# Seven block products for two tiles' q and k, with block sums on GpSimd

## The chip, the cores and the metric

The kernel runs on one core of a Trainium2 chip. The metric is the device time of one execution in microseconds. Times come from repeated runs; the profile is one further execution, in which every instruction was recorded.

## The reference, cut to what matters

The input x has 16 sequences of 1024 rows of 512 numbers, all fp32. One layer of linear attention and one gated feed-forward layer follow each other, each with a residual and a layer norm:

```python
qkv = x @ Wqkv.T + bqkv
q, k, v = jnp.split(qkv, 3, axis=-1)
q, k = rmsnorm(q, gq), rmsnorm(k, gk)          # then 16 heads of 32, rotated by position
qf, kf = relu(rope(q)), relu(rope(k))
vk  = einsum('bhlp,bhld->bhpd', vpad, kf)      # per sequence; vpad is v and a column of ones
res = einsum('bhpd,bhld->bhlp', vk, qf)
attn = res[..., :-1] / (res[..., -1:] + EPS_LIN)
x = layernorm(x + rmsnorm(attn @ Wout.T + bout, gout))
...
out = sigmoid(xr @ W_r.T) * (square(relu(xk @ W_k.T)) @ W_v.T)
x = layernorm(x + out)
```

Here xr and xk are mixes of each row of x with the row before it.

## The kernel before, in words

The rows are cut into N = 128 tiles of 128 rows, eight tiles to a sequence (a "block" below). Every fp32 matrix product is made of three fp32r products: each operand is split into a high half (a copy to fp32r, on ScalarE) and a low half (operand minus high half, on VectorE or GpSimd), and high x high, high x low and low x high are summed in PSUM. A product of 128 rows, 512 input columns and 512 output columns is therefore 4 x 3 = 12 matmuls of 512 columns.

The first stage walks over the tiles. For each, `slot` (L813; `early`, L775, for the first eight tiles) does this:

- loads the transposed tile xt and splits it (`split_x`, L329: copy L332, subtraction L333 giving xl); loads the plain tile xn and splits it (`split_xn`, L342: L347, L348);
- makes q and k, 12 matmuls each (`proj`, L422, matmul L433), into PSUM banks that ScalarE has filled with the bias before (`seed`, L357, through `seeded`, L160);
- takes the sum of squares on ScalarE (L459) and rotates on VectorE (`rope`, L455: two multiplications with tables, L465 and L466, and an addition with halves swapped, L467). q goes to DRAM (q_d). For k follow the mean square (L474), its power -1/2 on GpSimd (`rsqrt`, L147), the relu as high half kh and as fp32 (L478, L479) and the low half kl (L480);
- adds k's columns up over the block on GpSimd (`add_keys`, L484: acc, L489 and L491), and k-transposed times x on TensorE, 12 matmuls into four PSUM banks that stay open for the block (`add_kx`, L493, L509).

After a block, `finish_a`, `finish_s`, `finish_b` and `finish_c` (L519 to L602) make from these sums the 512x512 matrix m that takes q to the output projection of that sequence, and store it to DRAM (m_d). The rotation tables lie in DRAM (tab_d) and are loaded for each tile into four buffers (`rope_table`, L373, load L386). All loads are issued on SP's queue, in the order of the program.

From tile 30 on, every eighth tile also carries one output tile of the attention layer: q comes back from DRAM (`load_q`), is divided (`part_q`, L229) and transposed (`part_qt`, L244), multiplied with m (`part_m`, L260) and normalized with the residual (`part_y`, L290). Eight output tiles are made so in the first stage; the first four stay in SBUF, the others go to DRAM (x1_d). A block with such a tile is called woven below, the others bare.

The order in the first stage is set by the framework's scheduler, which gives every instruction a place on its engine; `in_order` (L107) fixes an engine's order to that of the program, for TensorE and GpSimd up to tile 7 and for TensorE again from the last tile on.

The second stage starts at L880: it loads the feed-forward weights (`load_w`), transposes four tiles of x at a time (`turn`, L892), mixes neighbouring rows, and runs the three feed-forward products, with the rest of the attention's output tiles between them. It begins with four turns of x tiles 0 to 3 while the last sums of the first stage are finished (L970 to L1021).

Of the kernel before, what the change touches and what calls it, by code (L numbers as in the profile page):

```python
# [22 lines left out]
NQ = 3  # L23
FIRST, STEP = 30, 8
# [9 lines left out]
def kernel(  # L34
# [121 lines left out]


# [37 lines left out]
    def load_m(b, c):  # L195
        n = NC_ * b + c + (2 if b > 0 else 0)
        ms[b, c] = ring("m", n, NC_, 2, [P, 2, DIM], F32R, f"mb{b}{c}")
        nc.sync.dma_start(out=f32(ms[b, c]), in_=m_d[b][:, :, c, :])
# [7 lines left out]
    def load_q(j):  # L206
        qs[j] = tp.tile([P, DIM], F32, tag="q", bufs=3, name=f"q{j}")
        nc.sync.dma_start(out=qs[j], in_=q_d[j])

    def x_tile(j):  # L210

        k = j % 11
        if k < NT:
            return tp.tile([P, DIM], F32, tag="x", bufs=NT, name=f"x{j}")
        if k < 2 * NT:
            return own["x"].tile([P, DIM], F32, tag="x", bufs=NT, name=f"x{j}")
        return tp.tile([P, DIM], F32, tag="xw", bufs=3, name=f"x{j}")

    def load_x(j, src=None, early=False):
        if early and j >= NT:  # L220
            xs[j] = tp.tile([P, DIM], F32, tag="xw", bufs=3, name=f"xw{j}")
        else:
            xs[j] = x_tile(j)
# [5 lines left out]
    def part_q(j):  # L229

# [4 lines left out]
        V.reduce_sum(den, heads(pr), AX.X)  # L235
        rs = rstd_all[:, j, 0:1]
# [7 lines left out]
    def part_qt(j):  # L244
        q = qs.pop(j)
        ps = bank(f"psqt{j}")
        transposes(ps, [q[:, c * P : (c + 1) * P] for c in range(NC_)])
        ps = groups(ps)
        th = wp.tile([P, NC_, P], F32R, tag="qth", bufs=2, name=f"qth{j}")
        tl = wp.tile([P, NC_, P], F32R, tag="qtl", bufs=2, name=f"qtl{j}")  # L250
        S.copy(th, ps)
        V.tensor_sub(tl, ps, f32(th))
# [24 lines left out]
    def layernorm_steps(xt, sm, name):  # L277
# [4 lines left out]
        S.activation(junk(name), xt, AF.Square, bias=nm, accum_out=sq)  # L282
        V.tensor_scalar(sq, sq, 1.0 / DIM, LN_EPS, ALU.mult, ALU.add)
# [10 lines left out]
    def part_y_steps(j, ps):  # L294
# [4 lines left out]
        S.activation(junk(f"y{j}"), ps, AF.Square, accum_out=ss)  # L299
        V.tensor_scalar(ss, ss, 1.0 / DIM, RMS_EPS, ALU.mult, ALU.add)  # L300
# [9 lines left out]
    with ExitStack() as a_ctx:  # L310
# [13 lines left out]

        def load_xt(i):
            xts[i] = wa.tile([P, NC_, P], F32, tag="xt", bufs=2, name=f"xt{i}")
            return nc.sync.dma_start(out=xts[i], in_=xt[i])

        def split_x(i):  # L329
            xh[i] = wa.tile([P, NC_, P], F32R, tag="xh", bufs=2, name=f"xh{i}")  # L330
            xl[i] = wa.tile([P, NC_, P], F32R, tag="xl", bufs=2, name=f"xl{i}")
# [10 lines left out]
        def split_xn(i):  # L342

# [3 lines left out]
            S.copy(h, w)  # L347
            V.tensor_sub(l, w, f32(h))  # L348
            xn[i] = h, l

        w_qk = {h: ca.tile([P, NC_, 2 * DIM], F32R, name=f"wqk_{h}") for h in "hl"}
# [21 lines left out]
        def rope_table(i, j):  # L373
# [4 lines left out]
            for n in (1, 0):  # L378
                if i == 2 and n == 1:

                    tb = tp.tile([P, DIM], F32, tag="x", bufs=NT, name=f"tab{j}{n}{i}")
                else:
                    tb = wa.tile([P, DIM], F32, tag=f"tab{j}{n}", name=f"tab{j}{n}{i}")
# [38 lines left out]
        def proj(i, j, by_part=False):  # L422
# [3 lines left out]
            cols = slice(j * DIM, (j + 1) * DIM)  # L426
# [5 lines left out]
            for n, ((a, b), c) in enumerate(order):  # L432
# [3 lines left out]
                    rhs=w_qk[b][:, c, cols],  # L436
# [16 lines left out]
        acc, ros, sums = {}, {}, {}  # L453

        def rope(i, j, ps):  # L455

            if j == 0:
# [5 lines left out]
            r = wa.tile([P, DIM], F32, tag=f"ro{j}", bufs=1 + j, name=f"ro{j}{i}")  # L463
            t2 = wa.tile([P, DIM], F32, tag="t2", name=f"t2{j}{i}")
            V.tensor_mul(t2, ps, tab.pop((i, j, 1)))  # L465
            V.tensor_mul(ps, ps, tab.pop((i, j, 0)))  # L466
            V.tensor_add(halves(r), halves(ps), halves(t2)[:, :, ::-1, :])  # L467
            if j == 0:
                q_d[i] = dram.tile([P, DIM], F32, name=f"q_d{i}")
                nc.sync.dma_start(out=q_d[i], in_=r)  # L470
                return

            ss = sums.pop(i)
            V.tensor_scalar(ss, ss, 1.0 / DIM, RMS_EPS, ALU.mult, ALU.add)  # L474
            rsqrt(rstd_all[:, i, :], ss)
            kh = tk.tile([P, DIM], F32R, tag="kh", bufs=2, name=f"kh{i}")
            kl = tk.tile([P, DIM], F32R, tag="kl", bufs=2, name=f"kl{i}")
            S.activation(kh, r, AF.Relu, scale=rstd_all[:, i, 1:2])  # L478
            S.activation(r, r, AF.Relu, scale=rstd_all[:, i, 1:2])  # L479
            V.tensor_sub(kl, r, f32(kh))  # L480
            state[i] = kh, kl
            ros[i] = r

        def add_keys(i):  # L484

            b, t = divmod(i, 8)
            if t == 1:
                acc[b] = tx.tile([P, DIM], F32, tag="acc", name=f"acc{b}")
                G.tensor_add(acc[b], ros[i - 1], ros[i])  # L489
            if t > 1:  # L490
                G.tensor_add(acc[b], acc[b], ros[i])  # L491

        def add_kx(i):  # L493

            kh, kl = state.pop(i)
            h, l = xn.pop(i)
            b, t = divmod(i, 8)
            if t == 0:
# [6 lines left out]
            if t == 7 and i < N - 1:  # L505

                order = [(three[n], c) for c in range(NC_) for n in (0, 1, 2)]
            for (n, a, r), c in order:
# [4 lines left out]
                    start=(t == 0 and n == 0),  # L513
                    stop=(t == 7 and n == 2),
# [4 lines left out]
        def finish_a(b):  # L519

            kx = tx.tile([P, NC_, NC_, 2, P], F32R, tag="kx", name=f"kx{b}")
            for c, ps in enumerate(ps_kx.pop(b)):
                S.copy(kx[:, c, :, 0, :], groups(ps))
                V.tensor_sub(kx[:, c, :, 1, :], groups(ps), f32(kx[:, c, :, 0, :]))  # L524
            fin[b] = kx

        def split_keys(b):
            a = acc.pop(b)
            m = te.tile([P, 2, DIM], F32R, tag="m", bufs=2, name=f"ma{b}")
            S.copy(m[:, 0, :], a)  # L530
            V.tensor_sub(m[:, 1, :], a, f32(m[:, 0, :]))
            return m

        def finish_s(b, m=None):

            m = split_keys(b) if m is None else m
# [672 lines left out]
```

## Time and profile before

| | us |
|---|---|
| median of 3 runs | 2704.09 (2704.01 to 2704.91) |
| the profiled execution's span, first to last instruction | 2703.0 |
| first stage, up to the last of k's products with x | about 1197 |
| busy: VectorE | 2172.3 |
| busy: ScalarE | 1881.4 |
| busy: GpSimd | 697.4 |

The page names the engines PE (TensorE matmuls), PEld (its weight loads), DVE (VectorE), ACT (ScalarE), POOL (GpSimd) and SP (which issues the DMAs). A busy time is the time in which at least one of the engine's instructions was running, so two instructions that overlap count once. A group's row reads: line, engine, operation, output <- inputs, shapes, count | busy time, mean duration in ns | idle time of the engine just before, and what ended it. In a row of a window of time, each engine's busy time is followed by its number of instructions, then come the granted TensorE clock, the busy share of the DMA engines and GB/s. A row of the timeline starts with the start and the duration in us.

### The profile page before, as it was taken

How to read it: one execution, taken by the hardware profiler on the slowest of the kernel's cores; microseconds unless marked ns; L12 is line 12 of the kernel's file. 1: busy time of each engine (PE TensorE's matmuls, PEld its weight loads, DVE VectorE, ACT ScalarE, POOL GpSimd, SP SyncE). 2: the span in 40 equal slices, each digit the busy share in tenths (PEclk: the TensorE clock that was granted, in tenths of full speed). 3: DMA queues.
4: the chain of work that ended last, by engine and by line, in shares of the span. 5: the costliest groups of instructions: out<-in, count | busy, mean ns of one | idle time of the engine just before them, and what ended most of it. 6: DMA issues, size and time to landing. Idle time of an engine off the chain costs nothing.

```text
span 2703.0 us, 40210 instructions
## 1 busy us (share of the span) xinstructions
PE 2687.1 (99%) x12572; PEld 2231.5 (83%) x12572; DVE 2172.3 (80%) x4884; ACT 1881.4 (70%) x3820; POOL 697.4 (26%) x800
## 2 busy tenths in 40 slices
PE   9999999999999999999999999999999999999998
PEld 7888888888888888887888888888888888888887
DVE  8888888877887788776888888888888888888874
ACT  6666666666666566657787777778777777777775
POOL 5222222222222222234322222222222222222221
PEclk9999999999999999999999999999999999999999
DMA  7788787877777778754232322223132222313210
GB/s 260 238 266 260 260 268 259 264 231 232 229 232 229 255 248 254 245 197 147 92 119 59 109 94 93 85 90 116 59 109 94 89 90 91 113 59 110 74 55 36
DMA packets 232159, 433.28 MB, mean 160 GB/s; under 512 B 24693, under 2 KB 25205, under 8 KB 231945
## 3 DMA queue, kind: packets, MB, share of 16 engines
q1 hardware_dynamic: 231508, 430.05, 49.5%
q8 instruction: 99, 1.62, 0.2%
q14 instruction: 116, 0.94, 0.1%
q10 hardware_dynamic: 436, 0.66, 0.1%
HBM read 314.19 MB, written 116.42 MB: 159 GB/s over the span
## 4 chain that ended last, share of the span: by engine, by line
PE 62%; DVE 1%; ACT 1%; DMA 0%; issue 0%; POOL 0%; POOLq 0%; SPq 0%; DVEq 0%; ACTq 0%
PE psr L183 13%; PE psv L183 13%; PE psk L183 12%; PE psy L183 12%; PE psk L433 3%; PE psq L433 3%; PE pskx L509 3%; PE pst L168 2%; PE psqt L168 2%; PE pskv L556 0%; PE psm L598 0%; DMA q<-q_d 0%; DVE x L1089 0%; DVE mixk L905 0%; PE pskv L564 0%
## 5 line engine op out<-in xcount | busy, mean ns | idle before, releaser
L183 PE MATMUL psk<-mkh,w_k 128*128 128x512 f32 x1024 | 332.6, 396 | 0.8 <-DVE kx L524 0.7
L183 PE MATMUL psv<-w_v,kah 128*128 128x512 f32 (+1 forms) x1032 | 321.8, 393 | 0.0
L183 PE MATMUL psr<-w_r,mrh 128*128 128x512 f32 x1024 | 319.9, 398 | 0.7 <-ACT r L958 0.7
L183 PE MATMUL psy<-mb,qth 128*128 128x512 f32 x1024 | 320.0, 389 | 0.0
L491 POOL TENSOR_TENSOR acc<-acc,ro 128x512 f32<-128x512 f32 x96 | 155.8, 1623 | 268.3 <-ACT ro L479 211.3
L183 PEld LDWEIGHTS psy<-mb,qth 128*128 128x128 f32 x1024 | 191.9, 188 | 39.6
L183 PEld LDWEIGHTS psk<-mkh,w_k 128*128 128x128 f32 x1024 | 191.2, 188 | 40.1 <-DVE kx L524 1.0
L183 PEld LDWEIGHTS psr<-w_r,mrh 128*128 128x128 f32 x1024 | 189.3, 189 | 38.3 <-ACT r L958 1.1
L183 PEld LDWEIGHTS psv<-w_v,kah 128*128 128x128 f32 x1032 | 188.9, 188 | 36.4
L921 POOL TENSOR_TENSOR mkl<-mixk,mkh 128x512 fp32r<-128x512 f32 x127 | 166.2, 1309 | 186.4 <-ACT mkh L919 186.4
L147 POOL TENSOR_TENSOR rstd_all<-ss,mhalf 128x2 f32<-128x2 f32 x128 | 91.1, 712 | 473.2 <-DVE ss L474 465.1
L433 PE MATMUL psq<-wqk_h,xh 128*128 128x512 f32 x512 | 200.7, 392 | 0.7 <-ACT wqk_h L671 0.6
L183 PE MATMUL psv<-w_v,kal 128*128 128x512 f32 (+1 forms) x516 | 200.7, 389 | 0.0
L433 PE MATMUL psk<-wqk_h,xh 128*128 128x512 f32 x512 | 199.0, 390 | 0.9 <-ACT psk L360 0.9
L183 PE MATMUL psy<-mb,qtl 128*128 128x512 f32 x512 | 199.8, 390 | 0.0
L183 PE MATMUL psk<-mkl,w_k 128*128 128x512 f32 x512 | 199.8, 390 | 0.0
L433 PE MATMUL psq<-wqk_l,xh 128*128 128x512 f32 x512 | 198.9, 389 | 0.0
L433 PE MATMUL psq<-wqk_h,xl 128*128 128x512 f32 x512 | 198.8, 389 | 0.0
L433 PE MATMUL psk<-wqk_h,xl 128*128 128x512 f32 x512 | 198.8, 389 | 0.0
L433 PE MATMUL psk<-wqk_l,xh 128*128 128x512 f32 x512 | 198.8, 389 | 0.0
L183 PE MATMUL psr<-w_r,mrl 128*128 128x512 f32 x512 | 197.2, 395 | 0.0
L147 POOL TENSOR_TENSOR yrs<-yss,mhalf 128x1 f32<-128x1 f32 x128 | 70.1, 548 | 392.6 <-DVE yss L300 286.6
(203 smaller groups left out, 7165.9 us busy)
## 6 DMA issues: line engine op xcount, KB each, us to landing
tab<-tab_d SPq DMA_DIRECT2D x480, 256.0 KB
xt<-in_xt_dram SPq DMA_DIRECT2D x128, 256.0 KB
xn<-in_x_dram SPq DMA_DIRECT2D x128, 256.0 KB
q_d<-ro SPq DMA_DIRECT2D x128, 256.0 KB
m_d<-m SPq DMA_DIRECT2D x64, 512.0 KB
mb<-m_d SPq DMA_DIRECT2D x64, 512.0 KB
q<-q_d SPq DMA_DIRECT2D x128, 256.0 KB
out_dram<-x SPq DMA_DIRECT2D x127, 256.0 KB
```

Of the source, the lines that this page charges most:

```text
L147: G.tensor_tensor(dst, src, mhalf[:, 0 : src.shape[1]], ALU.pow)
L168: T.matmul(ps[:, n * P : (n + 1) * P], lhsT=b, rhs=ident, is_transpose=True, start=(n == 0), stop=(n == NC_ - 1), skip_group_check=True,)
L183: T.matmul(ps, lhsT=a[u][:, rows], rhs=b[w][:, cols], start=(afresh and c == 0 and k == 0), stop=(c == n - 1 and k == 2), skip_group_check ...
L433: T.matmul(ps, lhsT=a[i][:, c, :], rhs=w_qk[b][:, c, cols], start=(not seeds and n == 0), stop=(seeds and n == 3 * NC_ - 1), skip_group_ch ...
L491: G.tensor_add(acc[b], acc[b], ros[i])
L509: T.matmul(ps_kx[b][c], lhsT=a[:, c * P : (c + 1) * P], rhs=r, start=(t == 0 and n == 0), stop=(t == 7 and n == 2),)
L921: (V if by_v else G).tensor_sub(ml, m, f32(mh))
```

## The change

Two tiles a and b (of the same block) are taken together. Their transposed rows are each cut into two halves of 256 input columns (a1, a2 of tile a; b1, b2 of tile b, the names the diff gives to b's are contained in its sums), and the weights into q's and k's columns by the same two halves of input columns. The eight block products (two tiles, two halves, q and k; each six matmuls of 512 columns) become seven, p1 to p7, over sums and differences of the blocks.

- The weights' sums are made once, in tiles 2 and 3, on GpSimd (`mix_weights`), and split in tiles 3 to 6 (`split_weights`).
- For each pair GpSimd makes four block sums s1 to s4 and the low halves of all seven left operands, 128x256 each; ScalarE makes the high halves in seven copies.
- Three of the seven results are needed in more than one place: ScalarE copies z (p7) to SBUF (`z_out`) and the running sum to a second bank (`y_seed`), and VectorE makes three additions (`a_seed`: two, `k2_add`: one). The k of tile b is finished in SBUF and rotated there.
- The tables use one ring of five buffers in place of four single ones and come in the order q of a, k of b, q of b, k of a.
- The order of the whole first stage from tile 8 on is written out by hand: `pair` gives every step a time, and the steps are traced sorted by it. TensorE's order is fixed to that from tile 8 on.
- The output tile of a woven block now comes one block later in parts: q and m are loaded for each of them (`load_m(..., f"w{j}")`), and all eight go to DRAM and are loaded back at the start of the second stage, behind w_k and before w_r. One q tile, not three, is prepared ahead of the second stage, and several tiles change their place in SBUF.

```diff
-NQ = 3
-FIRST, STEP = 30, 8
+NQ = 1
+SOLO = 8
+WOVEN = 6
...
-                    tb = wa.tile([P, DIM], F32, tag=f"tab{j}{n}", name=f"tab{j}{n}{i}")
+                    tb = wa.tile([P, DIM], F32, tag="tab", bufs=5, name=f"tab{j}{n}{i}")
...
+        def mix_weights(c):
+            q1, k1, q2, k2 = (stage[j, n] for n in (c, c + 2) for j in range(2))
+            G.tensor_sub(q1, k1, q1)
+            G.tensor_sub(k1, k2, k1)
+            G.tensor_sub(k2, k2, q1)
+            G.tensor_sub(q2, q2, k2)
...
+        def block_sum(i, n):
+            a, b = xts[i], xts[i + 1]
+            one, two = slice(0, 2), slice(2, NC_)
+            u, v, op = {
+                "s3": (a[:, one, :], b[:, one, :], G.tensor_sub),
+                "s1": (b[:, one, :], b[:, two, :], G.tensor_add),
+                "s2": (parts.get((i, "s1")), a[:, one, :], G.tensor_sub),
+                "s4": (a[:, two, :], parts.get((i, "s2")), G.tensor_sub),
+            }[n]
+            t = parts[i, n] = wa.tile([P, 2, P], F32, tag="part", bufs=3, name=f"part{n}{i}")
+            op(t, u, v)
+
+        def split_block_steps(i, n):
...
+            S.copy(t[:, 0], src)
+            yield
+            G.tensor_sub(t[:, 1], src, f32(t[:, 0]))
+
+        def block_product(ps, blk, rhs, afresh=False):
+            order = [(u, w, c) for c in range(2) for u, w in ((0, "h"), (0, "l"), (1, "h"))]
+            for n, (u, w, c) in enumerate(order):
+                T.matmul(ps, lhsT=blk[:, u, c, :], rhs=rhs(w, c), ...)
...
+            def p7():
+                me["z"] = bank(f"psk{b}")
+                block_product(me["z"], blk("s3"), t_(3), afresh=True)
+            def p1():
+                block_product(first[a, 0], blk("a1"), lambda w, c: w_q[w][:, c, :])
+            def p2():
+                block_product(first[a, 0], blk("a2"), lambda w, c: w_q[w][:, 2 + c, :])
+            def p6():
+                block_product(me["y"], blk("s2"), t_(2))
+            def p5():
+                block_product(me["a"], blk("s1"), t_(1))
+            def p4():
+                block_product(me["y"], blk("a4"), t_(4))
+            def p3():
+                block_product(me["a"], blk("s4"), lambda w, c: w_k2[w][:, c, :])
+            def z_out():
+                me["k2"] = rope_tile(b, 1)
+                S.copy(me["k2"], me["z"])
+            def y_seed():
+                me["y"] = bank(f"psq{b}")
+                S.copy(me["y"], first[a, 0])
+            def a_seed():
+                me["a"] = bank(f"psk{a}")
+                V.tensor_add(me["a"], me["y"], b_qk[:, DIM : 2 * DIM])
+                V.tensor_add(me["y"], me["y"], me["k2"])
+            def k2_add():
+                V.tensor_add(me["k2"], me["k2"], me["a"])
...
+            at(t, p7)
+            t += 6 * U
+            at(t, z_out)
+            if was is not None:
+                at(t, was["p3"])
+                t += 6 * U
+            at(t, p1)
...
+            at(t, p6)
+            t += 6 * U
+            ty2 = t
+            at(t, a_seed)
+            at(t, kx_two)
+            t += (12 if r == 0 else 8) * U
...
+            at(t, p5)
+            t += 6 * U
+            ta2 = t
+            at(t, k2_add)
+            steps_at(rope_k_b(), t + 0.75, t + 0.8, t + 1.5, t + 2.2)
+            at(t, p4)
+            t += 6 * U
+            steps_at(rope_q_b(), t + 0.05, t + 1.6, t + 2.2, t + 2.95)
...
+            ts = t + 12 * U
+            steps_at(rope_k_a(), ts + 0.05, ts + 1.2, ts + 1.8, ts + 2.5)
...
+                at(t0 + 1.4, block_sum, n, "s3")
+                steps_at(later(split_block_steps, n, "s3"), t0 + 2.1, t0 + 2.5)
...
+        for i in range(SOLO, N, 2):
+            t = pair(i, t)
...
+            for _, _, fn, args in sorted(events, key=lambda e: e[0:2]):
+                fn(*args)
...
         load_w("k", cb)
+        for j in range(NT):
+            load_x(j, src=x1_d[j])
+        load_w("r", cb)
...
+        add_kx(N - 1)
         for c in range(3):
             turn(0, c, c)
...
-        add_kx(N - 1)
+        add_kx(N - 2)
```

In the diff, U = 0.2267 is the time in us that `pair` gives to one matmul, r is the pair's place in its block (0 to 3), and `kx_two` are the products of k with x of an earlier tile.

## The prediction

> **What bounds the kernel now.** I read the busy table of the page first, then the chain, then the wait list and the busy windows of the attention stage.
>
> ```profile
> span 2703.0 us, 40210 instructions
> ...
> PE 2687.1 (99%) x12572; PEld 2231.5 (83%) x12572; DVE 2172.3 (80%) x4884; ACT 1881.4 (70%) x3820; POOL 697.4 (26%) x800
> ```
>
> ```profile
> 2628.76 10.88 PE psk L183 x48
> 2674.24 10.88 PE psr L183 x48
> ```
>
> TensorE is busy all the way. The chain's rows give the price of one matmul of 512 columns: 10.88/48 = 0.2267 us. Work taken from TensorE is therefore worth its whole time, as long as another engine does not become the bound. For the attention stage the windows of two blocks of eight tiles answer that. The starts of the ksv copy (L541) give the block's period: 75.4 us where an output tile is woven in, 71.8 to 72.3 where none is.
>
> ```profile
> core 0: us, PE busy (x) PEld busy (x) DVE busy (x) ACT busy (x) POOL busy (x), PEclk, DMA share, GB/s
> 391.20:466.60 75.40, 75.40 (x351) 63.02 (x350) 62.67 (x117) 48.73 (x103) 18.04 (x17) 1.00 0.79 262
> 1062.20:1134.50 72.30, 72.30 (x336) 60.44 (x335) 57.34 (x101) 43.82 (x95) 17.43 (x15) 1.00 0.75 237
> ```
>
> TensorE has no gap at a granted clock of 1.00. VectorE is next: 62.7 of 75.4 us (83%) and 57.3 of 72.3 (79%). ScalarE has 35% left, GpSimd 76%, the DMA engines a fifth. Between 300 and 1000 us the wait list has 1.9 us in all in which matmuls or their weight loads waited for VectorE, so VectorE's idle fifth is real cover today.
>
> **The change part by part.** *Matmuls.* For each of 60 pairs seven products of six matmuls replace eight. The program orders hold 11004 and 10644 matmuls of 512 columns: 360 fewer, 360 x 0.2267 = 81.6 us. A block loses 24, or 5.4 us: TensorE needs 66.6 us (bare) or 70.0 (woven).
>
> *VectorE's own work.* Prices from the woven block:
>
> ```profile
> L480 DVE TENSOR_TENSOR kl<-ro,kh 128x512 fp32r<-128x512 f32 x8 | 7.0, 880 | 3.2 <-ACT ro L479 3.2
> ...
> L466 DVE TENSOR_TENSOR psk<-psk,tab 128x512 f32<-128x512 f32 x8 | 5.5, 691 | 0.0
> ...
> L348 DVE TENSOR_TENSOR xnl<-xn,xnh 128x512 fp32r<-128x512 f32 x8 | 5.5, 687 | 2.9 <-ACT xnh L347 2.9
> ...
> L333 DVE TENSOR_TENSOR xl<-xt,xh 128x512 fp32r<-128x512 f32 x8 | 5.5, 684 | 0.5 <-ACT xh L332 0.5
> ```
>
> One operation shows as 0.69 us, but neighbours overlap: L465 to L466 start 0.60 us apart, so each adds about 0.61 to the busy sum. Per block the eight xl subtractions leave for GpSimd (-4.9) and twelve additions come in (two to seed, one to finish, in each of four pairs: +7.3). Without contention a bare block then needs 57.3 + 2.4 = 59.7 us. The woven window also holds three weight splits (1.9) that fall in other blocks after the change: 62.7 - 1.9 + 2.4 = 63.2.
>
> *GpSimd's work and what it does to VectorE.* Per pair there are four block sums and seven low halves, all 128x256; no row shows this form. The memsets of 512 and 256 columns show how GpSimd scales:
>
> ```profile
> L698 POOL MEMSET sel_g<- 128x512 f32 x1 | 0.5, 528 | 0.0
> ...
> L697 POOL MEMSET sel_b<- 128x256 f32 x1 | 0.3, 315 | 0.0
> ```
>
> About 0.1 is fixed, so 1.29 us at 512 columns (L489, L491 undisturbed) makes 0.70 at 256; the ends are 0.64 (half) and 1.29 (all fixed). Per block: 44 x 0.70 + 8 x 1.29 (acc) = 41 us in which GpSimd reads two SBUF operands, 59% of 70 us; with the powers about 47. GpSimd itself has room. The trouble is what two rows of the timeline show:
>
> ```profile
> 501.44 1.29 POOL L491 TENSOR_TENSOR acc<-acc,ro 128x512 f32<-128x512 f32 x1 [2.83 <-ACT ro L479]
> ...
> 502.05 1.24 DVE L233 SCALAR_TENSOR_TENSOR pr<-q,ksb 128x512 f32<-128x512 f32 x1 [3.10 <-DMA q<-q_d]
> ...
> 513.04 0.69 DVE L480 TENSOR_TENSOR kl<-ro,kh 128x512 fp32r<-128x512 f32 x1 [1.39 <-ACT ro L479]
> 513.14 1.75 POOL L491 TENSOR_TENSOR acc<-acc,ro 128x512 f32<-128x512 f32 x1 [2.43 <-ACT ro L479]
> ```
>
> A VectorE operation with two SBUF operands that starts inside a GpSimd one is stretched (0.69 to 1.24), and the other way round GpSimd is (1.29 to 1.75). In 31 such kl starts the stretch is what GpSimd had left, less 0.14 us; operations with one operand in PSUM (L467) keep 0.69 inside the same spans. After the change 34 VectorE operations of a bare block have two SBUF operands (per pair two kl, two xnl, and the three of k's rotation that now starts in SBUF; six others), 37 of a woven one. Hit at random: 0.59 x (mean rest 0.425 - 0.14 = 0.285) = 0.17 us each, 5.7 and 6.2 us a block. Ends: what the two blocks carry today (1.7 and 2.2, their stretches in the trace), and every operation finding GpSimd at work, 0.285 each.
> The Trainium skill ("SBUF — State Buffer", Who interferes with whom) says that the later of the two fully blocks, and counts any GpSimd instruction that reads SBUF. By that a hit would cost the whole rest, 0.59 x 0.425 = 0.25 us, and the sum below would come out at 2712 us, a little slower than now; the rows end 0.14 us sooner, and xnl starts inside the small powers (L147) are not stretched at all (0.69), so I go by the rows.
>
> VectorE's demand: bare 59.7 - 1.7 + 5.7 + 1.2 (weight splits) = 64.9; woven 63.2 - 2.2 + 6.2 = 67.2. That is 97% and 96% of TensorE's need, where today's is 83%.
>
> *VectorE's idle time in its order.* The five table buffers are a ring, so the second table of the pair's last rotation may load only when the first of k's rotation before it has been read. Six VectorE operations (6 x 0.61 = 3.7 us) lie between, and a table took 4.4 us from issue to its sixteenth completion mark (median of 344 between 300 and 1100 us; nine in ten under 5.8): 0.7 us idle a pair; on SP the xn and xt loads and q's store queue behind the waiting table, each with some us to spare. kl waited 0.5 us per tile for ScalarE (37.9 us over 76); with a later VectorE I keep 0.2 a pair. A woven block also loads 2 MB of m again (mb landed in 6.6, not 4.4): 2.2 more. So 3.6 and 5.8 us a block. A late VectorE next holds the seeding additions, and behind them TensorE's products five and four, whose cover is 8 to 12 matmuls (1.8 to 2.7 us).
> Block: 64.9 + 3.6 = 68.5 (TensorE 66.6: 1.9 lost); 67.2 + 5.8 = 73.0 (70.0: 3.0 lost). Seven bare and eight woven blocks: 13 + 24 = 37 us.
>
> *Once only.* Before the first pair, TensorE waits for the square of tile 7's k (0.59 + 0.19), ss 0.16, the power 0.70, a block sum 0.70 and a 256-wide copy 0.40, then for a low half: 3 us. Eight more GpSimd subtractions (8 x 1.29) in tiles 2 and 3 outrun the 8.6 us tile by under 2 us: 1 us. At the end the first turns need four tiles from DRAM, queued on SP behind 2 MB of w_k; the kernel shows the same kind of wait today at the next turn:
>
> ```profile
> 1233.82 0.33 PE L168 MATMUL pst<-ident,x 128*128 128x128 f32 x1 [2.64 <-DMA x<-x_d]
> ```
>
> Here w_k landed 4.4 to 6.7 us after its issue, 1 MB more at 255 GB/s is 4 us, and some 22 to 34 matmuls (5.0 to 7.7 us) cover it: 2 to 6, taken as 4. Together 8 us. The block sums' own chain, ScalarE's seven narrow copies (for two wide ones and one seed fewer) and four more stores of x are hidden: ScalarE is at 65% and all of it is a pair ahead; without that cover a low half late by 0.7 us stops TensorE in each product.
>
> Sum: 2703.0 - 81.6 + 37 + 8 = 2666. The median lies 1.1 us over the profiled span: 2667.
>
> **The rivals.** *All of it hides:* GpSimd's operations fall where VectorE works on PSUM, at 0.10 us or less per operation VectorE stays inside TensorE's time. 2703 - 81.6 + 8 + 1.1 = 2630. For it: today TensorE waits 1.9 us in 700 for VectorE, although kl already meets acc often. Against it: 96% leaves little room to place anything.
> *The shared read decides:* in blocks, the loss is 7 x (34x - 3.8) + 8 x (37x - 3.2) = 534x - 52 us for x us per operation. From x = 0.24 on the 73.6 us left are eaten; at 0.285, every operation meeting GpSimd, the loss is 100: 2730, slower. For it: GpSimd waiting behind one VectorE operation goes next, so k's three in a row can each pay. Against it: GpSimd still rests for a third of the time.
> *The tables decide:* the DMA share rises from 0.79 to about 0.91 in woven blocks (2.1 MB more on 19.8, in 73 us), above the 0.85 that a block reached (279 GB/s, no stall). If tables land 0.7 us later, 2.8 us a block, 42 us: 2709, no change.
> That the change does not remove the matmuls is excluded by the counts.
>
> **How the numbers follow.** Forecast (2640 to 2695) 0.47; all hides 0.22; shared read 0.22; tables 0.09. The time is the forecast's, 2667. Its own range is 2640 to 2695; the range of 8 in 10 reaches into both sides, 2628 to 2722. A measurement here tells 0.2% (5.4 us) from no change. Faster: 0.47 + 0.22 + 0.02 of the tables = 0.71; within: 0.05 of the tables and 0.02 of the shared read = 0.07; slower 0.22.
>
> **What would show it.** TensorE's matmuls of 512 columns fewer by 360; VectorE over 90% busy up to about 1150 us, kl, xnl and k's rotation at means well over 0.69 us, PSUM operations still at 0.69; block periods near 68.5 and 73; TensorE waiting for VectorE's seeding additions. VectorE under 88% with gapless blocks would be the first rival; means over 0.95 us for two-SBUF operations the second; long waits of VectorE on tab the third. Wrong outright: TensorE waiting on GpSimd's low halves in each product.

## The result and the profile after

The changed kernel is slower, by 6%. The profiled execution is the fastest of its four (2863.0 us).

| | before | after |
|---|---|---|
| median, us | 2704.18 (4 runs) | 2870.52 (4 runs, 2863.01 to 2878.52) |
| ratio, 95% interval | | 1.0614 (1.0592 to 1.0636) |
| span of the profiled execution | 2703.0 | 2861.2 |
| start to the first ksv copy | 96.7 | 105.6 |
| mean period of the next six blocks (bare after the change) | 74.2 | 86.3 |
| mean period of the eight after them (woven after the change) | 74.1 | 81.7 |
| period of the last block | 73.7 | 90.8 |
| from there to the end | 1494.8 | 1493.2 |

The periods are those of the ksv copies' starts (L631 now). Of 158 us more in the span, 133 lie in the fourteen blocks, 17 in the last one, 9 at the start. The changed kernel's page, its span and its busy line:

```profile
span 2861.2 us, 40565 instructions
...
PE 2681.5 (94%) x12212; PEld 2171.1 (76%) x12212; DVE 2420.0 (85%) x4953; ACT 1936.5 (68%) x4068; POOL 1274.5 (45%) x1468
```

The 360 matmuls are gone (12572 to 12212 records), and TensorE, busy 99% of the span before, stands still for 6% of a longer one. The windows of a bare and of a woven stretch of the changed kernel:

```profile
200.00:600.00 400.00, 341.56 (x1445) 267.30 (x1445) 341.17 (x488) 220.68 (x504) 250.77 (x272) 0.95 0.67 215
700.00:1200.00 500.00, 447.77 (x1990) 352.62 (x1989) 469.27 (x720) 306.50 (x706) 336.41 (x373) 1.00 0.75 239
```

In the woven stretch VectorE is busy 94%, and little more fits in. In the bare one nothing is: TensorE and VectorE are both at 85%, ScalarE and GpSimd at 55 and 63%. So two things are to be explained: VectorE's larger work, and blocks in which every engine waits. Where TensorE stops is told by the changed kernel's list of waits, TensorE's alone, from 100 to 1340 us (total, times, longest):

```profile
PE psq L997 <- ACT psq L1077: 55.2, 51, 3.3
PE pskx L584 <- DVE kl L548: 32.7, 21, 2.3
PE psm L700 <- DVE m L705: 22.0, 16, 3.1
PE psk L997 <- DVE ro L1085: 14.5, 8, 1.9
PE psm L700 <- DVE ro L521: 9.4, 14, 0.7
```

Before the change the same list held 2.1 us (to 1210 us). (Counted from one matmul's start to the next, less its own 0.23 us, the first line is 65 us and the second 36; the expectations below use that count.) The longest line is a wait that the prediction does not name: p2 adds to the bank out of which ScalarE's copy (`y_seed`, L1077) has just begun to read. The timeline of a woven pair, rows of several engines, shows what comes before that stop:

```profile
909.09 0.69 DVE L1085 TENSOR_TENSOR ro<-ro,psk 128x512 f32<-128x512 f32 x1
...
909.57 0.74 POOL L990 TENSOR_TENSOR blks<-parts,blks 128x256 fp32r<-128x256 f32 x1 [1.86 <-ACT blks L988]
...
909.81 1.05 DVE L516 TENSOR_TENSOR t<-ro,tab 128x512 f32<-128x512 f32 x1
...
910.39 1.07 POOL L978 TENSOR_TENSOR parts<-xt 128x256 f32<-128x256 f32 x1
...
910.95 1.05 DVE L518 TENSOR_TENSOR ro<-ro,tab 128x512 f32<-128x512 f32 x1
...
911.42 1.19 POOL L990 TENSOR_TENSOR blks<-parts,blks 128x256 fp32r<-128x256 f32 x1
...
912.04 1.11 DVE L521 TENSOR_TENSOR ro<-ro,t 128x512 f32<-128x512 f32 x1
...
912.68 1.07 POOL L978 TENSOR_TENSOR parts<-parts,xt 128x256 f32<-128x256 f32 x1
...
913.08 0.70 DVE L534 TENSOR_SCALAR ss<-ss 128x2 f32<-128x2 f32 x1
...
913.86 0.70 POOL L148 TENSOR_TENSOR rstd_all<-ss,mhalf 128x2 f32<-128x2 f32 x1
...
914.59 0.72 ACT L541 ACTIVATE kh<-ro,rstd_all 128x512 fp32r<-128x512 f32 x1 [0.42 <-POOL rstd_all L148]
...
915.22 0.58 ACT L1077 COPY psq<-psq 128x512 f32<-128x512 f32 x1
...
915.85 0.50 PE L997 MATMUL psq<-wq_h,blka 128*128 128x512 f32 x1 [0.45 <-ACT psq L1077]
```

Two things are to be seen. From 909.8 on VectorE and GpSimd take turns: each operation starts inside one of the other engine and ends 0.54 to 0.61 us after that one's end, so all are 1.05 to 1.19 us long instead of 0.69 and 0.73. And the rows are one chain: p5 has ended at 909.1, and k2's addition, the rotation, the sum, the root, kh, the copy (which stands behind kh in ScalarE's queue) and p2 follow one another over 6.8 us. The next pair's p5 ended at 930.5, 14.6 us after p2 began, some 11 of them matmuls at 0.2267 us (3.4 us lie at half clock). There the chain is back where it began, after 21.4 us, and goes round again. Such a closed chain is called a ring below. A quarter of a block's period, the time that a pair has, is 21.6 us (bare) or 20.4 (woven).

### The profile page after: what moved, and what is told of

Same layout as the page of the kernel before. It is cut to its first block, busy times and chain, and to the rows that moved or that the text cites. A ratio compares the mean times of both kernels' runs of the same rounds, so it can differ in the third digit from the quotient of the medians.

```text
span 2861.2 us, 40565 instructions
## 1 busy us (share of the span) xinstructions
PE 2681.5 (94%) x12212; PEld 2171.1 (76%) x12212; DVE 2420.0 (85%) x4953; ACT 1936.5 (68%) x4068; POOL 1274.5 (45%) x1468
## 4 chain that ended last, share of the span: by engine, by line
PE 53%; DVE 1%; DMA 0%; issue 0%; ACT 0%; POOL 0%; POOLq 0%; SPq 0%; DVEq 0%; ACTq 0%
PE psr L188 12%; PE psk L188 12%; PE psv L188 12%; PE psy L188 11%; PE pst L173 2%; PE psqt L173 2%; PE pskx L584 1%; PE psq L997 0%; DMA x<-x_d 0%; DMA w_k<-w_dk 0%; PE psk L997 0%; PE pskv L651 0%; DVE pr L246 0%; DVE t L516 0%; PE psm L700 0%
## 5 line engine op out<-in xcount | busy, mean ns | idle before, releaser
L990 POOL TENSOR_TENSOR blks<-parts,blks 128x256 fp32r<-128x256 f32 x240 | 209.7, 874 | 217.0 <-ACT blks L988 215.6
L188 PE MATMUL psy<-mb,qth 128*128 128x512 f32 x896 | 280.0, 389 | 0.0
L997 PE MATMUL psq<-wq_h,blka 128*128 128x512 f32 x480 | 179.8, 415 | 56.7 <-ACT psq L1077 56.7
L148 POOL TENSOR_TENSOR rsa<-sqa,mhalf 128x1 f32<-128x1 f32 x128 | 79.6, 622 | 304.7 <-DVE sqa L304 293.8
L541 ACT ACTIVATE kh<-ro,rstd_all 128x512 fp32r<-128x512 f32 x128 | 92.7, 725 | 163.0 <-DVE ro L521 110.0
L188 PEld LDWEIGHTS psy<-mb,qth 128*128 128x128 f32 x896 | 168.0, 188 | 34.8
L148 POOL TENSOR_TENSOR rsf<-sqf,mhalf 128x1 f32<-128x1 f32 x128 | 70.2, 555 | 265.6 <-DVE sqf L304 240.4
L584 PE MATMUL pskx<-kl,xnh 128*128 128x512 f32 x512 | 149.7, 400 | 32.7 <-DVE kl L548 32.7
L188 PE MATMUL psy<-mb,qtl 128*128 128x512 f32 x448 | 174.8, 390 | 0.0
L988 ACT CAST blks<-parts 128x256 fp32r<-128x256 f32 x240 | 97.7, 407 | 108.1 <-PE psk L997 67.3
```

The costliest lines, as they stand in the source:

```text
L148: G.tensor_tensor(dst, src, mhalf[:, 0 : src.shape[1]], ALU.pow)
L188: T.matmul(ps, lhsT=a[u][:, rows], rhs=b[w][:, cols], start=(afresh and c == 0 and k == 0), stop=(c == n - 1 and k == 2), skip_group_check ...
L584: T.matmul(ps_kx[b][c], lhsT=a[:, c * P : (c + 1) * P], rhs=r, start=(t == 1 and n == 0), stop=(t == 8 and n == 2),)
L988: S.copy(t[:, 0], src)
L990: G.tensor_sub(t[:, 1], src, f32(t[:, 0]))
L997: T.matmul(ps, lhsT=blk[:, u, c, :], rhs=rhs(w, c), start=(afresh and n == 0), stop=(n == len(order) - 1), skip_group_check=True,)
```

## The experiments

All times stand beside 2870.5 for the changed kernel. The kernel before was run again beside each experiment, with medians of 2703.4 to 2704.2.

### First four: move the copy, move a load, leave GpSimd out

e1_p1_first makes p1 the first product of the pair, ahead of p7, so that the copy has 12 to 16 matmuls of cover:

```diff
+            at(t, p1)
+            t += 6 * U
             at(t, p7)
             t += 6 * U
...
             ta3 = t
-            at(t, p1)
-            t += 6 * U
             tx1 = t
             at(t, y_seed)
```

> Each pair now begins with the first block product (into the first tile's q bank) and makes the seventh after it; all the work is done, nothing else is moved. ScalarE's copy of the bank after the first product then lies under 12 to 16 matmuls (2.7 to 3.6 us) instead of none to 4. Theory A (TensorE loses the time in waits put newly into its fixed order): the 65.1 us that the second product waited for this copy, 52 times, go to under 10, and with some of the stops the half-clock stretches, 71.7 us of them before 1400 us, become fewer; 2870.5 falls by 65 to 95 us, to 2775-2805. Rival B (VectorE, slowed by GpSimd's reads, is the bound, and TensorE's stops only show its lateness): the wait moves from this copy to VectorE's kl, m and k2 sums, the time falls by under 20 us, to 2850 or more.

Measured: 2914.8 us (1.0786, 1.0765 to 1.0808), 44 slower. Both theories fall as they were put. The same stop grew with all its cover, in the list of waits of this run (TensorE, 100 to 1340 us):

```profile
PE psq L997 <- ACT psq L1077: 75.2, 44, 3.5
PE pskx L584 <- DVE kl L548: 42.7, 21, 2.3
```

In 34 of these 44 cases kh, ahead of the copy in ScalarE's queue, had waited for GpSimd's root. The place of p1 was not what made the copy late.

e2_xn_later:

```diff
-            steps_at(xn_b, t + 0.45, t + 2.8)
-            at(t + 2.85, load_xn, a)
+            steps_at(xn_b, t + 2.8, t + 4.4)
+            at(t + 4.45, load_xn, a)
```

> The split of the second tile's x (ScalarE's copy and VectorE's subtraction) is placed 2.35 and 1.6 us later in each pair, and the load that follows it 1.6 us later; all the work is done. Its load is issued only 3 to 5.5 us before its use now, and VectorE, which works in order, sits in the subtraction behind it. Theory A: ScalarE's wait for this load (49.9 us, 39 times between 200 and 1200 us) goes to under 15 us, the waits of the m products for VectorE's m subtraction (24.6 us) and part of those for kl (36.1 us) go with it; the time falls by 20 to 60 us, to 2810-2850. Rival B (VectorE's busy time is the bound, the order of its work is not): VectorE does the same work, the time stays within 10 us of 2870.

Measured: 2870.7 (1.0611, 1.0596 to 1.0627). No change in the time, but ScalarE's wait for the load did not go either (50.4 us from 200 to 1200 us; 49.9 in the changed kernel). So the run does not tell what that wait is worth.

e3_no_gpsimd:

```diff
-            t = parts[i, n] = wa.tile([P, 2, P], F32, tag="part", bufs=3, ...)
-            op(t, u, v)
+            parts[i, n] = u
...
-            G.tensor_sub(t[:, 1], src, f32(t[:, 0]))
...
-                    lhsT=blk[:, u, c, :],
+                    lhsT=(none if u else blk[:, 0])[:, c, :],
```

> GpSimd's block work is left out: the four block sums are replaced by the block they begin with, and the low halves of all seven blocks by one block of zeros made once; TensorE, ScalarE, VectorE and the transfers do as much as before. Theory A with the slow reads as one of its causes: VectorE's additions and subtractions from two SBUF tiles (kl 1255, xnl 1060, k's three steps 981 to 1049 ns between 400 and 1100 us) fall to 0.70-0.80 us, VectorE's busy time before 1400 us by 80 to 130 us, and the stops for kl, m, k2 and the rotation (about 100 us) go to under 35; the copy's 65 us stay; 2870.5 falls to 2755-2800. Rival B (this contention alone decides): the time falls to 2650-2690. Rival C (contention is small, the order of work decides): the additions get faster but the time falls by under 40 us, to 2830 or more.

Measured: 2823.6 (1.0441, 1.0421 to 1.0462). xnl and k's steps do fall to 0.68-0.69 us and VectorE's busy time in a block from 75-77 to 65-66, but the time hardly follows. The s3 cast now reads x directly and waits for its load, and what waits behind it on ScalarE is again the copy. This run's waits of ScalarE (200 to 1200 us) and of TensorE (100 to 1340 us):

```profile
ACT blks L989 <- DMA xt<-in_xt_dram: 63.2, 42, 4.9
```

```profile
PE psq L998 <- ACT psq L1078: 99.4, 43, 5.3
```

The edit took one cause away and, by these lines, made another, so it tells only that VectorE's pace and the time are not the same thing.

e4_both has the first two edits.

> The first and the second edit together (first product first; split of the second tile's x later); all the work is done. Theory A: the gains add up, with some more from the clock, 2720-2775; if the half clock comes from the stops, under 25 us of it are left before 1400 us. Rival B (VectorE bound): 2840 or more.

Measured: 2912.6 (1.0767, 1.0751 to 1.0783): e1 again.

### Second four: ScalarE's order

e5_copy_first puts the copy ahead of kh by a dependency:

```diff
             S.activation(kh, r, AF.Relu, scale=rstd_all[:, i, 1:2])
+            if copied:
+                not_before(last_of(mybir.EngineType.Activation), copied[0])
...
                 S.copy(me["y"], first[a, 0])
+                copied[:] = [last_of(mybir.EngineType.Activation)]
...
-            steps_at(kb, t + 0.9, t + 1.0, t + 3.2, t + 6.5)
+            steps_at(kb, t + 0.9, t + 1.0, t + 4.2, t + 6.5)
```

> Made after the first four runs, which put the copy's lateness on what stands ahead of it in ScalarE's queue: in 41 of the late cases of the changed kernel (50.0 us) it is kh of the pair before, which waits for GpSimd's inverse root. Here ScalarE's copy of the first product is ordered ahead of that kh; all the work is done, nothing else is moved by hand. Theory A (ScalarE's order): the second product's wait for the copy falls from 65 us to under 20, the time by 35 to 75 us, to 2795-2835. Rival B (VectorE's lateness is the bound, the copy is where it happens to show): kh and kl come later by what the copy gained, the stops for kl grow from 36 us by 30 or more, and the time stays at 2850-2885.

Measured: 2943.7 (1.0889, 1.0868 to 1.091), slower than either theory. The stop did leave the copy, and came back larger (TensorE's waits, 100 to 1340 us):

```profile
PE pskx L586 <- DVE kl L550: 63.1, 55, 3.0
PE pskx L586 <- ACT kh L541: 45.4, 22, 3.6
...
PE psq L999 <- ACT psq L1079: 15.1, 14, 1.6
```

kh one copy later, with the next split of x slipped in ahead of kl, makes each pair 1.2 us longer (73 us in 60). A path that answers to a delay like that seems to have no slack.

e6_blocks_after (e5, and three casts later):

```diff
-                steps_at(later(split_block_steps, n, "s2"), ty2 + 0.1, ty2 + 1.1)
-                steps_at(later(split_block_steps, n, "s1"), ta2 + 0.1, ta2 + 1.0)
-                steps_at(later(split_block_steps, n, "s4"), t + 0.6, t + 1.0)
+                steps_at(later(split_block_steps, n, "s2"), t + 0.1, t + 0.5)
+                steps_at(later(split_block_steps, n, "s1"), t + 0.15, t + 1.05)
+                steps_at(later(split_block_steps, n, "s4"), t + 0.6, t + 1.35)
```

> As the run before, and the casts of the blocks s2, s1 and s4 are placed after the last product of the pair; ScalarE sits in front of their buffers (86 us of waits for TensorE's products between 200 and 1200 us) with what is queued behind them. All the work is done. Theory A (any wait in ScalarE's queue comes out at TensorE): 5 to 30 us less than the run before. Rival (those waits are slack): within 6 us of the run before; or slower by 5 to 20 us, where the low halves, now three on GpSimd at once, hold up the inverse root.

Measured: 2949.1 (1.0897, 1.0877 to 1.0917), e5 within its spread. ScalarE's waits for block buffers are slack.

e7_no_gpsimd_copy_first is e3 with e5's dependency, for the casts too.

> The run without GpSimd's block work again (low halves and sums left out), with the copy ahead of kh and of the block casts, which there waited for x. The 113 us of waits for the copy should go to under 25. Theory A (ScalarE's order and VectorE's slowed operations together make the whole loss): 2650-2710, the chain of TensorE work nearly closed before 1340 us. Rival C (there is a third cause, as in transfers or banks): 2750 or more. Rival B (contention alone): the same as without the order, 2810-2830.

Measured: 2850.2 (1.054, 1.0519 to 1.0561). In the count of the expectations the copy's waits went from 113 to 15 us, as expected; 63 us for kl came in their place. VectorE does much the same work in a block here (63 and 65 us) as in e13 below (66 and 67), which is 73 us faster: with nearly the same work of VectorE the time differs, so the order and the waits count.

e8_p1_and_copy is e1 with e5's dependency and the casts of s3 and a1 after the copy (t0 + 4.2 and 4.4 for t0 + 2.1 and 2.6).

> The first product made first, the copy ahead of kh, and the casts of s3 and a1 placed after it; all the work is done. Theory A: the copy then has 12 to 16 matmuls and nothing ahead that waits for GpSimd; its wait is under 10 us, and the time 10 to 40 us under the run with the copy first alone, 2765-2815. Rival B: as the run with the first product first, 2880 or more, with the stops at kl.

Measured: 2866.9 (1.0596, 1.0578 to 1.0614), the changed kernel's time, with 81 us of stops at kl (same count) for the 65 at the copy. The stop that was taken from TensorE at one place came back at another.

### Third four: shorten the ring

e9_kx_after_p6 (e10: with e5's order besides, kl kept ahead of the split; e11: on e8's order):

```diff
-            at(t, next, kx_one)
-            at(t + 8 * U, next, kx_one, None)
-            t += 12 * U
...
             at(t, p6)
             t += 6 * U
             ty2 = t
-            at(t, a_seed)
+            at(max(t, tq + 2.65), a_seed)
+            at(t, next, kx_one)
+            at(t + 8 * U, next, kx_one, None)
+            t += 12 * U
...
             at(t, kx_two)
...
```

> After eight runs a new theory. Followed back from TensorE, the changed kernel's chain of waits between 200 and 600 us is TensorE for only 25%, against 88% before; it runs in a ring from pair to pair: p5, VectorE's k2 addition, the rotation, the sum, GpSimd's root, ScalarE's kh (and, behind it, the copy that p2 waits for), VectorE's kl, TensorE's key products, p6, p5 of the next pair. Here the twelve key products of the second tile stand after p6 instead of before it, which takes p6 and the products woven in ahead of it out of the ring; all the work is done. Theory L (the ring's length is the pair's time): the stops for kl go from 36 to under 12 us, but the ring through the copy is left, so the time falls by 10 to 50 us, to 2820-2860. Rival B (VectorE's sum of work): within 12 us of 2870.

> As the run before, with the copy ordered ahead of kh, and kh, k and kl of the second tile ordered ahead of the next split of x (which had slipped in front of them in the run with the copy first alone); all the work is done. Both ways round the ring are then shorter. Theory L: 2740-2815. Rival B: 2850 or more. If the order alone made the earlier run slow and there is no ring, this is where the copy's 65 us come back: 2790-2810, and the run before shows no gain.

> As the run with the first product first, the copy ahead of kh and the casts later (2867 us), with the twelve key products after p6; all the work is done. There the stops had moved to kl (81 us) and kh (25 us). Theory L: these go to under 30 together, the time to 2730-2800, the lowest of this call. Rival B: 2850 or more.

e12_no_root:

```diff
+            rk = mhalf[:, 0:1] if i > SOLO and i % 2 else rstd_all[:, i, 1:2]
-            S.activation(kh, r, AF.Relu, scale=rstd_all[:, i, 1:2])
+            S.activation(kh, r, AF.Relu, scale=rk)
...
```

> The changed kernel, with kh and k of each pair's second tile scaled by a constant instead of the inverse root (the norm of that tile is left out); all other work is the same, the root is still made. This takes the wait for the sum and for GpSimd's root, 1 to 2 us, out of the ring and out of ScalarE's queue in front of the copy. Theory L: 1.0 to 1.5 us less in each of 60 pairs, 2780-2815. Rival B (VectorE's work, or GpSimd's reads by themselves): less than 15 us, 2855 or more.

| | us | ratio, interval | bare block | woven block |
|---|---|---|---|---|
| e9 | 2843.2 | 1.0517 (1.05 to 1.0535) | 80.0 | 83.1 |
| e10 | 2848.0 | 1.0531 (1.0515 to 1.0547) | 80.8 | 83.4 |
| e11 | 2841.6 | 1.0504 (1.0486 to 1.0521) | 79.1 | 84.8 |
| e12 | 2832.9 | 1.0477 (1.0456 to 1.0498) | 80.2 | 81.9 |

In e9 to e11 the woven tiles' q is turned before it is divided, which changes their part of the output but not the work. All four gain 22 to 38 us. A bare block is 5.5 to 7.2 us shorter, a woven one 0.2 to 3.1 us longer. So the ring's length counts in the bare blocks; e12 takes the root out of the ring and out of ScalarE's queue in front of the copy at once, and does not part the two. What was expected of e10 to e12 (55 us and more) was too much, since the woven half of the stage gains nothing. In e12 VectorE is busy 93% of a woven block, which leaves little to gain; in e9 to e11 it is 88 to 89%, and what holds their woven blocks is not shown.

### Last three: the reads alone

e13_thin keeps every wait, the order and GpSimd's time, and takes the wide reads away:

```diff
-            op(t, u, v)
+            G.memset(t, 0.0)
+            G.memset(t, 0.0)
+            op(t[:, :, 0:4], u[:, :, 0:4], v[:, :, 0:4])
...
-            G.tensor_sub(t[:, 1], src, f32(t[:, 0]))
+            G.memset(f32(t[:, 1]), 0.0)
+            G.memset(f32(t[:, 1]), 0.0)
+            G.tensor_sub(t[:, 1, :, 0:4], src[:, :, 0:4], f32(t[:, 0, :, 0:4]))
```

> The changed kernel, in which each of GpSimd's eleven block operations of a pair is replaced by two fills of the same tile and the subtraction or addition of 4 columns of each 128: it waits for what it waited for and takes about its 0.7 us, but reads next to nothing (the block sums and low halves are left out but for 4 columns). Theory R (VectorE's additions from two SBUF tiles, 0.9 to 1.35 us instead of 0.69, are the main loss): kl to 0.85-1.0 (GpSimd's key additions still read), xnl and k's three steps to under 0.76, the block periods from 82-88 us to 72-77, the time to 2700-2770. Theory L alone (the ring of waits, with any durations): 2830 or more. If the fills slow VectorE as much as the reads did, the means stay over 0.9 us and nothing is told.

Measured: 2777.3 (1.0274, 1.0253 to 1.0294), 93 us less and 7 over the range expected. VectorE's groups from 700 to 1200 us, first of the changed kernel, then of this run:

```profile
L548 DVE TENSOR_TENSOR kl<-ro,kh 128x512 fp32r<-128x512 f32 x43 | 58.1, 1352 | 1.7
L378 DVE TENSOR_TENSOR xnl<-xn,xnh 128x512 fp32r<-128x512 f32 x50 | 54.9, 1097 | 1.6 <-ACT xnh L376 1.6
...
L516 DVE TENSOR_TENSOR t<-ro,tab 128x512 f32<-128x512 f32 x24 | 24.6, 1023 | 0.4
...
L534 DVE TENSOR_SCALAR ss<-ss 128x2 f32<-128x2 f32 x48 | 18.1, 377 | 1.0 <-ACT junk L510 1.0
...
L516 DVE TENSOR_TENSOR t<-psk,tab 128x512 f32<-128x512 f32 x24 | 16.3, 681 | 0.2
```

```profile
L548 DVE TENSOR_TENSOR kl<-ro,kh 128x512 fp32r<-128x512 f32 x45 | 49.7, 1104 | 6.1 <-ACT ro L545 6.1
L378 DVE TENSOR_TENSOR xnl<-xn,xnh 128x512 fp32r<-128x512 f32 x52 | 37.5, 720 | 5.5 <-ACT xnh L376 5.5
...
L534 DVE TENSOR_SCALAR ss<-ss 128x2 f32<-128x2 f32 x50 | 29.5, 590 | 3.9 <-ACT junk L510 2.1
L516 DVE TENSOR_TENSOR t<-psk,tab 128x512 f32<-128x512 f32 x25 | 25.9, 1034 | 0.2
...
L516 DVE TENSOR_TENSOR t<-ro,tab 128x512 f32<-128x512 f32 x25 | 17.2, 687 | 0.4
```

GpSimd is as busy as before, and xnl and k's steps are back at 0.69 to 0.72; kl still meets GpSimd's key additions, which still read. The run has a slowdown of its own, too: 13 of the 50 ss operations, each beside five fills in a row, took 1.43 to 1.46 us, and the multiplication behind them in VectorE's queue (t<-psk above) 1.35. So its 93 us are more likely too little than too much for the reads. The windows of this run:

```profile
200.00:600.00 400.00, 372.78 (x1640) 294.34 (x1639) 347.19 (x560) 250.90 (x575) 278.86 (x772) 0.98 0.77 244
700.00:1200.00 500.00, 464.65 (x2075) 367.25 (x2073) 427.40 (x743) 318.24 (x733) 335.69 (x946) 1.00 0.78 249
```

VectorE falls from 94% to 85% in the woven stretch, and now no engine is at its limit there. Blocks take 76.5 (bare) and 78.6 us.

e14_thin_ring has the same thin operations on e15's order.

> The same thin block operations (sums and low halves left out but for 4 columns) in the order with the shorter ring: first product first, the copy ahead of kh, key products after p6, q's transposes after these. Theory R: with VectorE at its full pace the ring has slack and its order no longer matters, within 25 us of the run before. Theory L: 30 to 70 us below the run before.

Measured: 2774.1 (1.0262, 1.0241 to 1.0282), within 4 us of e13: blocks of 74.1 and 79.7.

e15_ring is e11 with the transposes of q moved behind the key products, which makes it whole:

```diff
-            if r == 3 and j is not None:
-                qt = later(part_qt_steps, j)
...
             at(t + 2.85, load_xn, a)
+            if r == 3 and j is not None:
+                qt = later(part_qt_steps, j)
...
```

> The order with the shorter ring by itself, all the work done. In the three runs with the key products after p6, q of the first tiles was turned before it was divided (that part of their output is changed); here the transposes stand after the key products. Theory L's share is what this gains on 2870: 20 to 40 us, all of it in the blocks before 640 us (86 to 79 us each), none in the woven ones, where VectorE is over 90% busy: 2830-2855.

Measured: 2836.2 (1.0494, 1.0476 to 1.0512), 34 us less than the changed kernel: 79.2 us a bare and 83.0 us a woven block, for 86.3 and 81.7. It is the fastest whole version of the change, and still 132 us over the kernel before.

## Why the prediction was wrong

**The matmuls.** Right: 360 fewer.

**The share of GpSimd's reads: the step that failed.** The prediction let an operation of VectorE meet GpSimd by chance and took "Hit at random: 0.59 x (mean rest 0.425 - 0.14 = 0.285) = 0.17 us each, 5.7 and 6.2 us a block". Measured between 700 and 1200 us, kl lost 0.66 us, xnl 0.41, k's three steps 0.21 to 0.33, and even the 2-column ss 0.21; with kvtl and q's division 84 us in 500, that is 13.8 us a woven block for 6.2. The timeline says why: it is not chance. In it GpSimd's queue holds four block operations in a row while k's three steps run, the engine that was made to wait goes next, and every operation pays. The second rival had this mechanism, and its sign ("means over 0.95 us"), but not its size: its upper end was 0.285 us. The Trainium skill ("SBUF — State Buffer", Who interferes with whom) says that a VectorE instruction with two SBUF inputs contends with a GpSimd instruction that reads SBUF. The alternation in the timeline agrees. The prediction priced this on rows in which GpSimd had one operation at a time.

**A block as VectorE's work and its idle time.** In the prediction's own terms:

| us a block | bare, forecast | bare | woven, forecast | woven | e13 bare | e13 woven |
|---|---|---|---|---|---|---|
| VectorE busy | 64.9 | 74.8 | 67.2 | 76.7 | 66.4 | 67.1 |
| VectorE idle | 3.6 | 11.5 | 5.8 | 5.0 | 10.1 | 11.5 |
| period | 68.5 | 86.3 | 73.0 | 81.7 | 76.5 | 78.6 |

The busy term is 9.5 to 9.9 us too small. In a woven block 7.6 of it are the reads (13.8 for 6.2), and e13, with these reads gone, takes 8.4 and 9.6 us of VectorE's time away. That it comes out near the forecast is in part luck: the forecast has 5.7 and 6.2 us for reads in it, and e13 has the slow kl and ss instead. The idle term is the second step that failed. It counted the tables, kl and m, each against its own cover, and no path through several queues. The ring of 21 us was not looked for. VectorE's idle time is 8 us over the forecast in a bare block, and the runs that shorten the ring (e9 to e12) make that block 5.5 to 7.2 us shorter.

When the reads are gone, a woven block has 5.7 us of idle time over the forecast as well. That this is the ring is not shown. The longest of VectorE's waits there (e13, 640 to 1260 us, some eight blocks) are for a table, for GpSimd's key addition and for q's store, which both still read the buffer that VectorE writes next:

```profile
DVE psk L518 <- DMA tab<-tab_d: 16.6, 10, 2.7
DVE ro L521 <- POOL acc L556: 15.4, 13, 1.2
DVE ro L521 <- DMA q_d<-ro: 12.4, 8, 2.7
```

The first is 2.1 us a block, for which the forecast had 2.8; the other two have no term in it. The gains do not add up: the reads alone are 93 us, the order alone 34, both together 96.

**The edit costed at nothing.** ScalarE's new work stood under "hidden", since "ScalarE is at 65% and all of it is a pair ahead". That holds for the seven narrow copies. It does not hold for the wide y_seed, which the prediction has at most as one of the seeds that it counts ("one seed fewer"): it stands between p1 and p2 of the same pair, and TensorE waits for it there. It is the longest line of the list, but e5 and e8, which took most of it away, were no faster: the stop came back at kl and kh. So it was a place where the loss showed, not a loss of its own.

**Once only.** 8 us were forecast, 4 of them at each end. The start took 8.9 more, and the last block 9.1 more than the woven ones before it; 6.1 us of that are TensorE's waits for x's tiles from DRAM, the prediction's 2 to 6.

**The other rivals.** All of it hides: it needed 0.10 us or less for each operation, and 0.21 to 0.66 were lost. The tables: VectorE waited 3.7 us for them between 640 and 1260 us of the changed kernel, so no; they count only when VectorE is faster (16.6 us in e13). TensorE waiting for low halves, the sign of an outright error, was not seen in any block.

**Left open.** With neither the block operations' reads nor the longer ring (e14), 70 us over the kernel before remain. So what the experiments show is 96 us, less than half of the 204 us between the forecast and the result, and it does not account for the sign: without it the change would still be 2.6% slower. The other 107 us over the forecast lie mainly in the idle term. VectorE's work in e14 is below the forecast (63.6 and 64.8 us a block), its idle time 10.6 and 14.9 us for 3.6 and 5.8. Its longest waits (640 to 1260 us) and three of the longest stops of TensorE (100 to 1340 us) in e14:

```profile
DVE ss L534 <- ACT junk L510: 34.2, 23, 1.7
DVE psk L518 <- DMA tab<-tab_d: 26.6, 10, 4.6
DVE m L707 <- ACT m L705: 21.3, 14, 3.4
```

```profile
PE pskx L586 <- DVE kl L550: 18.9, 11, 2.3
PE psqt L173 <- DVE ro L521: 18.3, 8, 2.5
PE psks L630 <- ACT junky L320: 14.1, 8, 2.3
```

The longest of VectorE's waits is for ScalarE's sums of squares (junk), to which the prediction gave nothing. No run took one of these waits away, so which of them costs time is not shown.

## What to carry to other kernels

When work moves to GpSimd beside a VectorE that is some 80% busy, as here, ask what GpSimd's queue holds while each VectorE operation with two SBUF operands runs: if it is never empty, price every one of them as a turn taken (0.2 to 0.66 us here), not as a chance hit. When the margin of the bounding engine is a few per cent, follow one item through all the queues and back to its start, and compare that length with the period; busy shares do not show it. And a stop on the list of waits is a place, not a cause: order one wait away, and if the stop comes back elsewhere, look for the ring.

## What the hardware showed besides

The granted clock. Windows of the changed kernel around a stop, each one 3.4 us long; the last three figures are the clock, the DMA share and GB/s:

```profile
397.30:400.70 3.40, 1.26 (x6) 0.86 (x5) 3.21 (x4) 1.55 (x5) 2.50 (x3) 1.00 0.89 264
400.70:404.10 3.40, 3.40 (x9) 2.67 (x8) 1.13 (x2) 0.87 (x2) 0.00 (x0) 0.50 0.99 338
404.10:407.50 3.40, 2.25 (x10) 1.50 (x8) 3.12 (x5) 1.65 (x4) 2.43 (x2) 1.00 0.76 186
```

A 3.4 us stretch with 1.26 us of matmuls is followed by one at half clock, in which matmuls start 0.43 us apart. Between 62 and 1357 us this happened for 71.7 us, 36 us of full-clock time at most, all in multiples of 3.41 us, 47.8 of them in the bare blocks; before the change it happened once between the start and the last microseconds, at 1234.9 us. On the grid of these stretches, every one of the 17 after which the clock went down in the changed kernel had TensorE busy 49% or less. Three others at 47 to 50% were not followed by half clock, and in e15 three at 54% were, so the line lies near one half and is not sharp. e13 had 41.0 us at half clock, so at most some 15 us of its gain came by way of the clock (half of the 31 us less). The Trainium skill ("TensorE: Matmul & The Clock Gate", What's actually happening) gives this window and a return to half rate after an idle one; here a window about half idle was enough, so that a stop of 2 us can be paid nearly twice.

GpSimd's fills did not slow VectorE's wide operations with two SBUF operands (0.69 us for k's steps in e13). They did slow the 2-column ss, 0.16 us where nothing of GpSimd's ran beside it before the change: 0.59 on average in e13, 1.45 beside five fills in a row, with what stood behind it in the queue.
